# Second-conv results of the last image kept in SBUF, and the last stage's blocks in a mixed order

## The chip, the cores and the metric

The kernel runs on one core of a Trainium2 chip. The metric is the device time of one execution in microseconds (us). Three runs of the kernel before took 4049.6, 4058.78 and 4061.14 us; the median is 4058.78. The profiled execution spans 4055.7 us.

## The reference

Two layers run on x of shape (4, 128, 128, 128): four images of 128 channels and 128 x 128 pixels. Layer 0 is a windowed attention block followed by a depthwise-convolution MLP; it is not touched here. Layer 1 is a residual block with quantized 3x3 convolutions, and the change is in its last third:

```python
identity = x
out = act_quant(x)
out = conv3x3(out, weight_quant(w1))
out = batchnorm(out, gamma1, beta1)     # mean and variance over batch and pixels
out = act_quant(out)
out = conv3x3(out, weight_quant(w2))
out = batchnorm(out, gamma2, beta2)
return out + identity
```

The batchnorm is what shapes the kernel: no output of the second convolution can be scaled before the mean and variance over all four images are known.

## The kernel before, in words

The channels lie on the 128 partitions. Layer 1 cuts each image into 32 blocks of 4 rows, so that a block is 128 channels x 512 pixels: [...]256 KB in float32. Four images make 128 blocks. A convolution of one block (`conv3x3`, L783) is nine matmuls of 128x128 weights on 128x512 pixels, all in fp8, accumulated in one of four PSUM tiles (`ps_c`, L773).

Layer 1 runs in three stages after layer 0.

- The first-conv stage (L835 to L863) finishes layer 0 block by block, writes its result to HBM as the identity (`id_d`), quantizes it, convolves it with `wq[0]`, takes the statistics of the result (`stats_of`, L793) and copies the result out of PSUM (L829). For images 0 to 2 the copy goes on to HBM (`c1_d`). For image 3 it stays in SBUF, in `c1_s` (L800), 64 KB on each partition.
- The second-conv stage (L885 to L898) takes each first-conv result, from HBM or from `c1_s`, applies batchnorm and relu on ACT (L889), quantizes it in two DVE instructions (L890, L891) into padded fp8 images `q2` that stay in SBUF, and convolves each block with `wq[1]`, for the statistics alone (L896, L898): the results are thrown away. The last statistics feed the batchnorm's scale and shift (L900), a chain of small DVE and POOL instructions.
- The last stage (L913 to L922) convolves all 128 blocks a second time with the same `q2` and `wq[1]`. ACT applies scale and shift to the PSUM tile and writes `z` to SBUF (L918), DVE adds the identity (L919), and a DMA writes the block to the output (L920). The identity blocks come from HBM by `load_id` (L905).

`z`, the identity tile `idt` and the tiles of the second-conv stage come from the pool `ew` with three buffers each (L871). Identity loads are asked for two blocks ahead. Loads and writes of this stage are all issued by SyncE, in order, from one queue.

The order of the instructions on each engine in these stages is not the order of the program text: a scheduler arranges them when the kernel is built. For the second-conv stage it puts on ACT first all 96 relus that read loaded blocks and then all 32 that read `c1_s`. In the last stage SyncE's instructions alternate, one write and one load. Earlier parts (the attention) are arranged by hand; they don't concern the change.

Of the kernel before, what the change touches and what calls it, by code (L numbers as in the profile page):

```python
# [10 lines left out]
AF = mybir.ActivationFunctionType  # L11
# [3 lines left out]
P = 128  # L15
# [6 lines left out]
RB = 4  # L22
NBLK = P // RB
# [18 lines left out]
def layers(  # L42
# [29 lines left out]
    nc = tc.nc  # L72
    B = x.shape[0]
# [65 lines left out]
    with (  # L139
# [19 lines left out]
        for w in (wqkv, wp0.rearrange("p h m -> p (h m)")):  # L159
            n = w.shape[1]  # L160
# [41 lines left out]
    wq, kscale = [], []  # L202
# [28 lines left out]
    with (  # L231
# [27 lines left out]
        for n in range(3 * 32):  # L259
            s, ro, eo = n // 32, n % 32 // 2, n % 2  # L260
            m = ms[n % 4]
# [25 lines left out]
    with ExitStack() as actx:  # L287
# [352 lines left out]
        def beside(t):  # L640

            one = ln1_chunks(t + 1) if t + 1 < T else []
            two = post_chunks(t - 1) if t else []
            if t >= 2:
                b, i = bands[t - 2]
                if i == 4:
                    todo.extend(conv_steps(2 * b))
                    share[0] = -(-len(todo) // 4)  # L650
                elif i == NR - 1:
                    todo.extend(conv_steps(2 * b + 1))
                    share[0] = -(-len(todo) // 5)
            conv = [todo.pop(0) for _ in range(min(share[0], len(todo)))]
            n = max(len(one), len(two), 1)
            conv_of = [conv[len(conv) * c // (2 * n + 2) : len(conv) * (c + 1) // (2 * n + 2)] for c in range(2 * n + 2)]
            steps = []
            for c in range(n + 1):
                first = one[c] if c < len(one) else [None] * 4
                second = two[c] if c < len(two) else [None] * 5  # L660
                before = two[c - 1] if 0 < c <= len(two) else [None] * 5
                steps += [first[0]]
                if c:
                    steps += [second[0], before[3], *conv_of[2 * c], first[1], second[1], before[4]]
                else:
                    steps += [*conv_of[0], first[1], second[0]]
                steps += [*conv_of[2 * c + 1]]
                if c:
                    steps += [second[2], first[2], first[3]]
                else:  # L670
                    steps += [first[2], second[1], first[3], second[2]]
            return [s for s in steps if s]
# [6 lines left out]
        with nullcontext() if safe else tc.manual_schedule(engines=MANUAL):  # L679
# [5 lines left out]
            for t in range(T):  # L685
# [3 lines left out]
                side, at = beside(t), 0  # L689
                for j in range(NR):  # L690
# [5 lines left out]
                    for half in range(2):  # L696
# [3 lines left out]
                        at = upto  # L700
# [10 lines left out]
    def batchnorm(stats, n, gamma, beta, ks, name):  # L711

        mv = const.tile([P, n, 2], F32, name=f"mv{name}")
        for h in range(n):
            nc.vector.bn_aggr(mv[:, h, :], stats[h].rearrange("p c s -> p (c s)"))
        return affine(mv[:, :, 0], mv[:, :, 1], n, gamma, beta, ks, name)
# [53 lines left out]
    st2 = const.tile([P, B * NBLK, 6], F32, name="st2")  # L770
# [4 lines left out]
    def padded(pool, name):  # L775
        q = pool.tile([P, QW, QW], F8, name=name)
        nc.gpsimd.memset(q[:, 0, :], 0.0)
        nc.gpsimd.memset(q[:, QW - 1, :], 0.0)
        nc.gpsimd.memset(q[:, 1 : QW - 1, 0:1], 0.0)
        nc.gpsimd.memset(q[:, 1 : QW - 1, QW - 1 :], 0.0)  # L780
        return q

    def conv3x3(q, w, k):  # L783
        pc = ps_c.tile([P, RB, P], F32, name="pc")
        for t in range(9):
            dy, dx = divmod(t, 3)
            nc.tensor.matmul(  # L787
                pc, w[:, t, :], q[:, k * RB + dy : k * RB + dy + RB, dx : dx + P],
                start=(t == 0), stop=(t == 8),
            )  # L790
        return pc

    def stats_of(st, n, pc):  # L793
        nc.vector.bn_stats(st[:, n, :], pc.rearrange("p r c -> p (r c)"))  # L794

    blocks = [(b, k) for b in range(B) for k in range(NBLK)]
# [3 lines left out]
    c1_s = q1p.tile([P, P * P], F32, name="c1_s")  # L800
# [69 lines left out]
    q2 = [padded(q1p, f"q1_{b}") for b in range(B)]  # L870
    ew = ctx.enter_context(tc.tile_pool(name="ew", bufs=3))  # L871
    firsts = {}

    def load_first(n):
        b, k = blocks[n]
        px = slice(k * RB * P, (k + 1) * RB * P)
        if b == B - 1:
            firsts[n] = c1_s[:, px]
            return
        firsts[n] = ew.tile([P, RB * P], F32, name="c1l")  # L880
        nc.sync.dma_start(out=firsts[n], in_=c1_d[b][:, px])

    load_first(0)
    load_first(1)
    for n, (b, k) in enumerate(blocks):  # L885
        if n + 2 < len(blocks):
            load_first(n + 2)
        a = ew.tile([P, RB * P], F32, name="a")
        nc.scalar.activation(a, firsts.pop(n), AF.Relu, bias=sh1, scale=sc1)  # L889
        nc.vector.tensor_scalar(a, a, 15.0, ROUND, ALU.min, ALU.add)  # L890
        nc.vector.tensor_scalar(  # L891
            q2[b][:, 1 + k * RB : 1 + (k + 1) * RB, 1 : 1 + P],
            a.rearrange("p (r c) -> p r c", c=P), ROUND, None, ALU.subtract, saturate=False,
        )
        if k:
            stats_of(st2, n - 1, conv3x3(q2[b], wq[1], k - 1))  # L896
        if k == NBLK - 1:
            stats_of(st2, n, conv3x3(q2[b], wq[1], k))  # L898

    sc2, sh2 = batchnorm([st2], 1, ga2, be2, kscale[1], "2")  # L900

# [3 lines left out]
    def load_id(n):  # L905
        b, k = blocks[n]
        t = ew.tile([P, RB * P], F32, name="idt")
        nc.sync.dma_start(out=t, in_=id_d[b][:, k * RB * P : (k + 1) * RB * P])
        idt[n] = t

    load_id(0)
    load_id(1)
    for n, (b, k) in enumerate(blocks):  # L913
        if n + 2 < len(blocks):
            load_id(n + 2)
        pc = conv3x3(q2[b], wq[1], k)
        z = ew.tile([P, RB * P], F32, name="z")
        nc.scalar.activation(z, pc.rearrange("p r c -> p (r c)"), AF.Identity, bias=sh2, scale=sc2)  # L918
        nc.vector.tensor_tensor(z, z, idt.pop(n), ALU.add)  # L919
        nc.sync.dma_start(  # L920
            out=out[b, :, k * RB : (k + 1) * RB, :].rearrange("c r w -> c (r w)"), in_=z
        )  # L922
# [3 lines left out]
def conv_seq_kernel(tc: tile.TileContext, *args: bass.AP):  # L926
    nc = tc.nc
    with tc.tile_pool(name="flag", bufs=1) as fp:
        flag = fp.tile([1, 1], mybir.dt.int32, name="flag")
        layers(tc, False, flag, *args)  # L930


        large = nc.values_load(flag[0:1, 0:1])
        with tc.If(large > 0):
            layers(tc, True, flag, *args)
# [34 lines left out]
```

## Time and profile before

The stages of layer 1, from the trace (us from the start of the span; busy times in us):

| stage | from | to | PE busy | ACT busy | DVE busy | DMA share, GB/s |
|---|---|---|---|---|---|---|
| first conv | 2940 | 3524 | 518.3 of 584 | 397.1 | 308.4 | 0.87, 285 |
| second conv, its beginning | 3524 | 3560 | 31.8 of 36 | 20.5 | 27.6 | 0.60, 177 |
| second conv, while blocks are loaded | 3560 | 3670 | 99.9 of 110 | 73.6 | 96.5 | 0.56, 165 |
| second conv, after the loads | 3670 | 3740 | 70.0 of 70 | 7.2 | 33.3 | 0.00, 1 |
| second conv, its end | 3740 | 3803 | 63.0 of 63 | 0.0 | 25.6 | 0.00, 1 |
| last stage | 3810 | 3850 | 40.0 of 40 | 17.0 | 15.2 | 0.87, 288 |
| last stage, near its end | 3950 | 4000 | 50.0 of 50 | 19.5 | 18.0 | 0.84, 270 |

The first `z` of the last stage starts at 3803.25 us, the last at 4046.82, and the span ends at 4055.7. In the second-conv stage nothing but TensorE limits the time from 3670 on, with the DMA engines idle.

How to read the views: a group's line names the kernel's line, the engine and operation, output and inputs, the shapes and the count; then busy time in us, mean ns of one, idle time before them and what ended it. In the waits a row gives who waited for whom, the total in us, how many times, and the longest. Chain and timeline give the start and length in us of each piece of work. In a table of stretches "PEclk" is the share of full clock that TensorE was granted, and the DMA share is the mean busy share of the core's 16 DMA engines.

### The profile page before, as it was taken

The page shows a single profiled execution, that of the slowest core. Times are in us where ns is not written, and L with a number is a line of the kernel's source. Part 1 is how long each engine was busy: PE and PEld are TensorE (multiplying, and loading weights), DVE is VectorE, ACT ScalarE, POOL GpSimd, SP SyncE. Part 2 cuts the span into 40 slices and gives each one's busy share as a digit, 9 for nine tenths or more (in the row PEclk, how much of TensorE's full clock was granted, in tenths as well). Part 3 has the DMA queues.
Part 4 walks back from the last instruction along what each step waited for, and adds up shares of the span by engine and source line. Part 5 has one row for each costly group of instructions (what it writes and reads, how often), then busy time and mean ns, then how long its engine had stood idle before and what let it go on. Part 6 is the DMA issues. An engine that isn't in the chain of part 4 may idle for free.

```text
span 4055.7 us, 87210 instructions
## 1 busy us (share of the span) xinstructions
PE 3762.9 (93%) x35916; PEld 1914.1 (47%) x35916; DVE 1826.5 (45%) x3358; ACT 2326.4 (57%) x3534; POOL 384.2 (9%) x1381
## 2 busy tenths in 40 slices
PE   7699999999999999999999999997688889999999
PEld 5355455555555555555545555553333333334444
DVE  5244444444444444444444444442245555685433
ACT  3367666666666666666666666653156667662233
POOL 0011110111110010111110111100011111100000
PEclk9999999999999999999999999998579999999999
DMA  1223266676656657655666764657888889760487
GB/s 39 108 62 80 73 135 149 146 143 152 148 116 141 148 134 159 150 140 110 150 147 139 160 146 118 144 129 162 182 255 300 295 297 304 231 199 1 137 271 250
DMA packets 782938, 643.68 MB, mean 159 GB/s; under 512 B 572736, under 2 KB 585664, under 8 KB 782528
## 3 DMA queue, kind: packets, MB, share of 16 engines
q1 hardware_dynamic: 782528, 637.98, 60.8%
q8 instruction: 286, 4.69, 0.5%
q14 instruction: 124, 1.02, 0.1%
HBM read 365.07 MB, written 272.76 MB: 157 GB/s over the span
## 4 chain that ended last, share of the span: by engine, by line
PE 76%; DMA 9%; ACT 4%; issue 3%; DVE 3%; POOL 2%; SPq 2%; ACTq 0%; POOLq 0%; DVEq 0%
PE po L615 14%; PE pc L787 12%; PE pm L496 9%; PE sc L561 8%; PE pm L306 6%; PE pm L382 6%; PE pm L313 6%; PE pm L437 5%; DMA cv<-cv_d 3%; PE pm L549 3%; PE pb L849 3%; PE pm L420 2%; PE pw L269 2%; DMA c1l<-c_d 2%; DMA u<-y_d 2%
## 5 line engine op out<-in xcount | busy, mean ns | idle before, releaser
L628 DVE RECIPROCAL rd<-po 128x256 f32<-128x256 f32 x324 | 569.6, 1758 | 633.4 <-PE po L615 633.4
L787 PE MATMUL pc<-q,wq 128*128 128x512 fp8e4 x3456 | 794.5, 382 | 23.3 <-DVE st L794 9.4
L569 ACT ACTIVATE pt<-sc 128x1024 f32<-128x1024 f32 x648 | 627.2, 1019 | 58.0 <-PE sc L561 47.1
L787 PEld LDWEIGHTS <-wq 128*128 128x128 fp8e4 x3456 | 337.4, 98 | 517.5 <-issue 151.6
L496 PE MATMUL pm<-u,w 40*32 40x256 f32 x12288 | 454.6, 410 | 57.4 <-DMA u<-y_d 44.7
L507 DVE BATCH_NORM_STATS2 st<-c 128x6 f32<-128x256 f32 x512 | 181.4, 414 | 469.4 <-ACT c L505 468.9
L561 PE MATMUL sc<-q,kr 32*128 32x256 f32 x5184 | 373.6, 401 | 0.0
L496 PEld LDWEIGHTS pm<-u,w 40*32 40x32 f32 x12288 | 258.7, 112 | 240.8 <-issue 112.2
L505 ACT COPY c<-pm 128x512 f32<-128x512 f32 x256 | 139.0, 588 | 386.8 <-PE pm L496 377.8
L615 PE MATMUL po<-pt,v 128*32 128x256 f32 x5184 | 346.9, 385 | 0.0
L615 PE MATMUL po<-pt,ones 128*32 128x256 f32 x5184 | 339.1, 379 | 0.0
L561 PEld LDWEIGHTS sc<-q,kr 32*128 32x128 f32 x5184 | 233.9, 184 | 218.7 <-issue 181.3
L313 PE MATMUL pm<-sq,avg 128*128 128x512 f32 (+1 forms) x576 | 281.9, 571 | 31.7 <-ACT sq L308 27.0
L443 ACT ACTIVATE y<-pm,bp 128x512 f32<-128x512 f32 (+1 forms) x288 | 183.4, 641 | 222.9 <-PE pm L437 111.9
L849 PE MATMUL pb<-ge,wp 128*128 128x512 f32 x512 | 265.6, 614 | 46.6 <-ACT ge L846 46.5
L382 PE MATMUL pm<-xn,wqkv 128*128 128x512 f32 (+1 forms) x576 | 269.2, 570 | 15.6 <-DVE xn L318 15.6
L437 PE MATMUL pm<-xn,wp 128*128 128x512 f32 (+1 forms) x576 | 268.9, 559 | 5.7 <-DVE xn L318 5.7
L841 ACT ACTIVATE ge<-cv,shift,scale 128x512 f32<-128x512 f32 x256 | 202.8, 844 | 111.2 <-DMA cv<-cv_d 107.2
L308 ACT ACTIVATE sq<-pm 128x512 f32<-128x512 f32 (+1 forms) x288 | 157.2, 546 | 187.8 <-PE pm L306 187.7
L794 DVE BATCH_NORM_STATS2 st<-pc 128x6 f32<-128x512 f32 x256 | 177.8, 696 | 189.3 <-PE pc L787 189.2
L918 ACT ACTIVATE z<-pc,shift,scale 128x512 f32<-128x512 f32 x128 | 99.3, 777 | 269.0 <-PE pc L787 130.1
L315 ACT ACTIVATE rstd<-pm,eps_t 128x512 f32<-128x512 f32 (+1 forms) x288 | 184.3, 640 | 120.3 <-PE pm L313 114.7
(143 smaller groups left out, 4026.0 us busy)
## 6 DMA issues: line engine op xcount, KB each, us to landing
u<-y_d SPq DMA_DIRECT2D x128, 528.0 KB
cv_d<-c SPq DMA_DIRECT2D x512, 128.0 KB
cv<-cv_d SPq DMA_DIRECT2D x128, 512.0 KB
y_d<-y SPq DMA_DIRECT2D x224, 264.0 KB
w<-dw_d SPq DMA_DIRECT2D x64, 768.0 KB
xfl<-xf_d SPq DMA_DIRECT2D x128, 256.0 KB
id_d<-y SPq DMA_DIRECT2D x128, 256.0 KB
idt<-id_d SPq DMA_DIRECT2D x128, 256.0 KB
```

Source lines behind the costliest of these rows:

```text
L306: nc.tensor.matmul(pc[:, :n], center, src(), start=True, stop=True)
L313: nc.tensor.matmul(pv[:, :n], avg, held["sq"][:, :n], start=True, stop=True)
L382: nc.tensor.matmul(pm[:, : n * P], wqkv[:, m * P : (m + 1) * P], held["xn"][:, : n * P], start=True, stop=True,)
L437: nc.tensor.matmul(pm[:, : n * P], wp0[:, h, :], held["xn"][:, : n * P], start=True, stop=True)
L496: nc.tensor.matmul(pc[half][32 * q : 32 * q + 32, j, :].rearrange("p (g x) -> p g x", g=4), wt[hs, c, s, :], ut[hs, :, c, s : s + 64], sta ...
L561: nc.tensor.matmul(sc[h // 2][:, h % 2, kc, :].rearrange("p (r c) -> p r c", c=RS), region(kr, j)[hs, kc * P : (kc + 1) * P], queries(j, h ...
L569: nc.scalar.activation(pt, sc[p], AF.Exp)
L615: nc.tensor.matmul(po[hs, m, :], ones if m else v[:, kc, hs], pt[h // 2][:, h % 2, kc, :], start=(kc == 0), stop=(kc == 1),)
L628: nc.vector.reciprocal(rd, po[:, 1, :])
L787: nc.tensor.matmul(pc, w[:, t, :], q[:, k * RB + dy : k * RB + dy + RB, dx : dx + P], start=(t == 0), stop=(t == 8),)
L841: nc.scalar.activation(ge[:, h, :].rearrange("p (r c e) -> p r e c", r=RB, e=2), cv[:, h, :].rearrange("p (r e c) -> p r e c", r=RB, e=2), ...
L849: nc.tensor.matmul(pb, wp2[:, h, :], ge[:, h, :], start=(h == 0), stop=(h == 1))
```

## The change

`c1_s`, the SBUF room of image 3's first-conv results, is free once the second-conv stage has read them. The change uses it again. When the second-conv stage convolves a block of image 3, ACT copies the result from PSUM to that block's place in `c1_s`. In the last stage image 3 is then not convolved again: ACT reads its blocks from `c1_s`. So that the kept blocks don't come all at the end, the last stage goes through an order in which three computed blocks of images 0 to 2 are followed by one kept block of image 3, 32 times over. It is meant to relieve TensorE in the last stage.

```diff
+    def second_conv(n):
+        b, k = blocks[n]
+        pc = conv3x3(q2[b], wq[1], k)
+        stats_of(st2, n, pc)
+        if b == B - 1:
+            nc.scalar.copy(
+                c1_s[:, k * RB * P : (k + 1) * RB * P], pc.rearrange("p r c -> p (r c)")
+            )
...
         if k:
-            stats_of(st2, n - 1, conv3x3(q2[b], wq[1], k - 1))
+            second_conv(n - 1)
         if k == NBLK - 1:
-            stats_of(st2, n, conv3x3(q2[b], wq[1], k))
+            second_conv(n)
...
-    load_id(0)
-    load_id(1)
-    for n, (b, k) in enumerate(blocks):
-        if n + 2 < len(blocks):
-            load_id(n + 2)
-        pc = conv3x3(q2[b], wq[1], k)
+    order = [m for k in range(NBLK) for m in (*range((B - 1) * k, (B - 1) * (k + 1)), (B - 1) * NBLK + k)]
+    load_id(order[0])
+    load_id(order[1])
+    for at, n in enumerate(order):
+        b, k = blocks[n]
+        if at + 2 < len(order):
+            load_id(order[at + 2])
+        if b < B - 1:
+            pc = conv3x3(q2[b], wq[1], k).rearrange("p r c -> p (r c)")
+        else:
+            pc = c1_s[:, k * RB * P : (k + 1) * RB * P]
         z = ew.tile([P, RB * P], F32, name="z")
-        nc.scalar.activation(z, pc.rearrange("p r c -> p (r c)"), AF.Identity, bias=sh2, scale=sc2)
+        nc.scalar.activation(z, pc, AF.Identity, bias=sh2, scale=sc2)
```

In the changed kernel the copy stands at L879, the relu at L898, and `z`, the add and the write at L933 to L935.

## The prediction

> **What bounds the kernel now.** I read the chain of waits of the last 265 us first, since the change touches only the end of the program. Columns: start in us, length in us, what.
>
> ```profile
> 3789.86 256.93 PE pc L787 x1184
> 4046.79 0.02 issue
> 4046.82 0.79 ACT z L918
> 4047.60 0.02 issue
> 4047.62 0.69 DVE z L919
> ```
>
> The last stage is one unbroken run of matmuls on TensorE, then one block's scale-and-shift (ACT), one add (DVE), and 8.9 us from the last z at 4046.82 to the end of the span at 4055.7, in which the last writes land. So TensorE sets the end. Two groups of the page size the work:
>
> ```profile
> L918 ACT ACTIVATE z<-pc,shift,scale 128x512 f32<-128x512 f32 x128 | 99.3, 777 | 269.0 <-PE pc L787 130.1
> L794 DVE BATCH_NORM_STATS2 st<-pc 128x6 f32<-128x512 f32 x256 | 177.8, 696 | 189.3 <-PE pc L787 189.2
> ```
>
> ACT and DVE each need under 0.8 us of a block. Next the waits of the last stage, its first 35 us and then the rest (waiter, releaser, us in total, times, longest):
>
> ```profile
> ACT z L918 <- DMA out_dram<-z: 13.5, 12, 2.1
> DVE z L919 <- ACT z L918: 10.6, 12, 2.1
> DVE z L919 <- DMA idt<-id_d: 9.9, 6, 2.7
> ACT z L918 <- PE pc L787: 5.8, 6, 1.2
> ```
> ```profile
> DVE z L919 <- ACT z L918: 136.0, 108, 1.6
> ACT z L918 <- PE pc L787: 125.5, 107, 1.2
> ACT z L918 <- DMA out_dram<-z: 1.5, 1, 1.5
> ```
>
> These two differ in kind, and the forecast rests on that. When the batchnorm is ready at 3803.25, TensorE has run four blocks ahead (four accumulators), so the first z's don't wait for matmuls. They wait for z buffers whose write hasn't landed (12 times) and for identity loads (6 times). Only when ACT has used up that lead is it TensorE that ends the wait, 107 times of 108. The first 25 us thus show the stage without its TensorE limit. In the timeline (start, length, instruction, idle before and releaser):
>
> ```profile
> 3807.03 0.78 ACT L918 ACTIVATE z<-pc,shift,scale 128x512 f32<-128x512 f32 x1 [1.67 <-DMA out_dram<-z]
> ...
> 3828.63 0.78 ACT L918 ACTIVATE z<-pc,shift,scale 128x512 f32<-128x512 f32 x1 [0.66 <-DMA out_dram<-z]
> ...
> 3830.10 0.78 ACT L918 ACTIVATE z<-pc,shift,scale 128x512 f32<-128x512 f32 x1 [0.69 <-PE pc L787]
> ```
>
> The z at 3807.03 is the fourth, that at 3828.63 the sixteenth: 21.60 us / 12 = 1.80 us a block. Without the first step (2.44 us, the queue filling up; the fifth z starts at 3809.47) it is 19.16 / 11 = 1.74. From 3830.10 to 4046.82 the other 111 blocks take 216.72 us, 1.95 each: nine matmuls of 217 ns. Last, busy time by stretch (us; PE, PEld, DVE, ACT, POOL with counts; clock, DMA share, GB/s):
>
> ```profile
> 3300.00:3400.00 100.00, 89.32 (x298) 35.29 (x297) 51.90 (x90) 68.84 (x92) 13.52 (x22) 1.00 0.89 298
> 3807.00:3829.00 22.00, 22.00 (x104) 9.85 (x102) 8.31 (x12) 9.70 (x13) 0.00 (x0) 1.00 0.90 304
> 3838.00:4046.80 208.80, 208.78 (x963) 93.36 (x960) 74.11 (x107) 83.03 (x107) 0.00 (x0) 1.00 0.84 269
> ```
>
> At TensorE's pace the DMA engines already stand at 84% and 269 GB/s. Freed of it they reach 90% and 304 GB/s, the level of the first-conv stage (298), which often waits for its loads. The room below TensorE is some 12%, not the 25% of matmuls that go.
>
> **What the Trainium skill says.** "DMA: Bandwidth & Descriptors", Anatomy of one DMA: about 2 us of a transfer are fixed, mostly the write's receipt (fitted there for the GpSimd path). The trace agrees in kind: the stage's first 256 KB write is issued at 3804.78 and frees its buffer at 3807.03, 2.25 us; under load issue to reuse is 2.8 to 5.3 us. "HBM Reference", Specifications: about 358 GB/s per core. The trace has 359 for one 4 us stretch (3807 to 3811) but holds 304 over 22 us; the measured figure is used. "TensorE: Matmul & The Clock Gate", Part 1: the clock halves after an idle window of about 3.4 us. The trace has 0.50 from 2860 to 2980 us, where TensorE is idle a third of the time, and 1.00 from 3300 to 3400, where it is 89% busy.
>
> **The change, part by part.**
>
> 1. *Matmuls removed.* The last image's 32 blocks are not convolved again: 32 x 9 = 288 matmuls, 32 x 1.95 = 62.4 us of TensorE, all on the chain. TensorE then needs 96 x 1.95 = 187 us, or 5.86 us for each group of three computed blocks and a kept one (1.46 us a block).
>
> 2. *Copies added.* 32 ACT copies of 128x512 from PSUM in the second-conv stage. The same copy in the first-conv stage (L829) has a median of 577 ns: 18.5 us of ACT. ACT is idle there: between 3670 and 3740 it is busy 7.15 us, from 3740 to 3803 not at all, and the last image's convolutions fall at 3803 - 32 x 1.95 = 3741 and later. In program order each copy would stand ahead of the next relu (L889), and the relu's block feeds the next convolution, which would tie ACT to TensorE block by block; in the order as built all 128 relus come first and then the 32 copies, so nothing but copies is queued behind a copy that waits. Each copy follows its block's statistics (L829 does so too), so an accumulator is held 0.70 + 0.58 = 1.28 us after its last matmul; with four of them TensorE needs it back only after three more blocks, 5.9 us. The last copy runs beside the batchnorm, whose steps on DVE and POOL take from 3797.54 to 3803.15. Cost: nothing. The copy overwrites first-conv results that ACT has read by 3679.
>
> 3. *Loads and writes.* The same 128 loads and 128 writes of 256 KB, the same three buffers of each, the same alternation on the queue (write, load, write, load), only in another order of blocks. A kept block reads SBUF in place of PSUM: the relu from this buffer (L889) takes 808 ns against the 777 of z, 32 x 0.03 = 1 us, hidden under the waits.
>
> 4. *What sets the pace then.* A z buffer goes through ACT 0.78, DVE 0.69, then issue to reuse, mean 3.58 us over the ten writes issued from 3809.5 to 3824.9: with handovers about 5.15, and with a third to half a us of the waits for loads 5.3 for three blocks, 1.77. By bandwidth: 2 x 262,144 bytes at 304 GB/s are 1.72 us, at 298 1.76. By count, 1.74 to 1.80. I take 1.76; ends 1.68 (the 312 GB/s held from 3020 to 3060) and 1.86 (282 GB/s).
>
> Sum: the fourth z stays at 3807.03 (it waits for the first write, as now). The 128th comes 124 x 1.76 = 218.2 us later, at 4025.3, against 4046.8; the 8.9 us tail stays. Saved: 21.5 us. From 4058.8 that gives 4037; with 1.68 4027, with 1.86 4050. TensorE, needing 1.46 of 1.76 us, is 83% busy and has the rest to make up delays.
>
> **Rivals.**
>
> *A, the transfers keep up.* If the queue fills the DMA engines (304 / 0.90 = 338 GB/s), a block takes 1.55 us and the last z comes at 3807.03 + 192.2 = 3999: 48 us less, 4011. The 359 GB/s of one 4 us stretch speak for it; against it, 304 over 22 us with ACT already waiting for buffers, and 298 over a long stage that has larger loads.
>
> *B, a wait takes the matmuls' place.* Reads and writes come in bunches (2.9 us issue to reuse for one write, 5.3 for another 2.7 us later). If three buffers settle into the bad phase, a block costs about 1.95 us as now: 4058, no change. Nearby traffic that ran at 304 speaks against it.
>
> *C, slower.* TensorE now pauses in every group. If it lost half its clock for a third of the stage, three blocks would take 9 x 3 x 0.43 = 11.6 us, 2.9 for each of 43 blocks: 43 x 2.9 + 85 x 1.76 = 274 us against 250, so 24 us slower, 4083. The 0.50 clock before 2980 speaks for it; against it, the pauses would be 4 x 1.76 - 5.86 = 1.2 us, and the first-conv stage at 87 to 89% busy holds 1.00. A copy that blocked relus would end on this side too, but the order as built excludes it.
>
> **How the numbers follow.** Main case 78%, A 9%, B 8%, C 5%. The time is the main case's, 4037. The range goes from 4023, a little into A, to 4050, where B begins. Faster by over 0.3% (below 4046.6) is A and the main case up to 1.84 us a block: 0.86; within 0.3%: 0.09; slower: 0.05.
>
> **What would show it.** Right: the last stage's chain alternates z, add and DMA in place of one matmul run; ACT's z waits chiefly for the write of z and DVE for idt; DMA share near 0.90 and 295 to 312 GB/s up to the end; z spacing near 1.76 us; TensorE about 83% busy at clock 1.00; 32 copies from about 3741 with TensorE unbroken up to 3803, and the first z still at 3803. Wrong: gaps in TensorE before 3803 (step 2), a spacing near 1.46 with ACT waiting for pc (step 4, towards A) or near 1.95 at less than 280 GB/s (B), a clock below 0.9 (C).

## Result and profile after

The changed kernel takes 4039.66 us (median of six runs, 4026.91 to 4043.68), against a forecast of 4037 with a range of 4023 to 4050. With three more runs of the kernel before, its median is 4051.57. The ratio is 0.9958, with a 95% interval of 0.9938 to 0.9978: 17 us less, between 9 and 25. Both kernels scatter by more than 10 us, and part of that has nothing to do with the change. In the two profiled runs the first-conv stage starts at 2978.9 us before and at 2984.0 after, though the change touches no instruction ahead of it. So the stage itself is the finer measure.

The waits of the last stage (waiter, releaser, us in total, times, longest):

```profile
ACT z L933 <- DMA out_dram<-z: 100.7, 104, 2.5
DVE z L934 <- DMA idt<-id_d: 83.3, 61, 2.6
DVE z L934 <- ACT z L933: 55.0, 65, 2.6
...
PE pc L787 <- ACT z L933: 27.9, 34, 2.0
...
ACT z L933 <- PE pc L787: 3.3, 3, 2.2
```

Before, ACT waited 107 times of 108 for TensorE once the first 35 us were over. Now it does so three times in the whole stage, and 104 times it waits for a write to land and give back its z buffer. TensorE in turn waits for ACT to give back an accumulator. The instructions of z and the copies (duration min/median/max in ns, first and last start in us):

```profile
L933 ACT ACTIVATE z<-pc,shift,scale x96: 769/777/778, 3807.2 to 4030.0; 128x512 f32<-128x512 f32 x96
L933 ACT ACTIVATE z<-c_s,shift,scale x32: 812/812/815, 3811.5 to 4032.4; 128x512 f32<-128x512 f32 x32
L879 ACT COPY c_s<-pc x32: 585/585/586, 3741.0 to 3801.6; 128x512 f32<-128x512 f32 x32
```

From first to last z the stage takes 4032.4 - 3807.2 = 225.2 us, where it took 4046.8 - 3803.2 = 243.6. From the fourth z (3811.52) to the last (4032.39) a block costs 220.87 / 124 = 1.78 us.

Where these 1.78 us come from can be read off the single instructions (means over blocks 11 to 110). A z buffer's round is 0.79 us on ACT, 0.31 until its add starts (chiefly the wait for the identity load), 0.69 for the add, 0.03 to the issue of the write, and 3.49 from there until ACT fills the buffer again: 5.31 us. An identity buffer's round is as long, within 0.01: 0.69 for the add, 0.42 to the issue of the next load, 4.19 from there to that load's add. Three buffers share a round, so a block takes 5.31 / 3 = 1.77 us. The queue hardly holds the writes back, as the 0.03 us show.

Busy time by stretch (us; PE, PEld, DVE, ACT, POOL with counts; clock, DMA share, GB/s):

```profile
3740.00:3803.00 63.00, 63.00 (x292) 28.23 (x291) 23.84 (x33) 18.73 (x32) 0.00 (x0) 1.00 0.00 1
...
3829.00:4032.00 203.00, 168.51 (x747) 72.39 (x746) 79.18 (x115) 90.31 (x115) 0.00 (x0) 0.99 0.91 296
```

The 18.7 us of copies leave TensorE unbroken. In the last stage it is busy 168.51 of 203 us, 83%, at a clock of 0.99, while the DMA engines move 296 GB/s at a share of 0.91. In the profiled pair 18.4 us come off the stage, 0.5 go to a longer tail (9.4 us for 8.9), and 4.0 to the later first z: 13.9, the difference of the two spans.

### The profile page after: what moved, and what is told of

Its sections match the earlier page's. It is cut to its first block, busy times and chain, and to the rows that moved or that the text cites. A ratio compares the mean times of both kernels' runs of the same rounds, so it can differ in the third digit from the quotient of the medians.

```text
span 4041.8 us, 86698 instructions
## 1 busy us (share of the span) xinstructions
PE 3712.2 (92%) x35628; PEld 1887.7 (47%) x35628; DVE 1825.2 (45%) x3358; ACT 2345.4 (58%) x3566; POOL 382.8 (9%) x1381
## 5 line engine op out<-in xcount | busy, mean ns | idle before, releaser
L787 PE MATMUL pc<-q,wq 128*128 128x512 fp8e4 x3168 | 737.4, 381 | 51.8 <-ACT z L933 27.9
L787 PEld LDWEIGHTS <-wq 128*128 128x128 fp8e4 x3168 | 308.7, 98 | 517.8 <-issue 190.6
L549 PEld LDWEIGHTS pm<-wqkv,yr 128*128 128x128 f32 x1296 | 193.6, 191 | 122.4 <-issue 117.5
```

The source lines that it names most:

```text
L549: nc.tensor.matmul(pv[:, c, :], region(yr, j)[:, c * P : (c + 1) * P], wqkv[:, 2 * P :], start=True, stop=True)
L787: nc.tensor.matmul(pc, w[:, t, :], q[:, k * RB + dy : k * RB + dy + RB, dx : dx + P], start=(t == 0), stop=(t == 8),)
```

## The experiments

What was open was why a block costs 1.78 us. The forecast had two counts for it that gave the same number, three buffers waiting for their own landings and DMA engines near their limit, and did not separate them. The diffs below are against the changed kernel unless another is named. "Stage" is the time from first to last z in the profiled run; each ratio is to runs of the kernel before on the same chip, with its 95% interval. The runs were made in three batches on three chips, so between batches compare stages and ratios, not times.

### The copies alone

```diff
-    order = [m for k in range(NBLK) for m in (...)]
+    order = list(range(len(blocks)))
...
-        if b < B - 1:
-            pc = conv3x3(q2[b], wq[1], k).rearrange("p r c -> p (r c)")
-        else:
-            pc = c1_s[:, k * RB * P : (k + 1) * RB * P]
+        pc = conv3x3(q2[b], wq[1], k).rearrange("p r c -> p (r c)")
```

> The 32 copies are made in the second-conv stage, but nothing reads them: the last stage convolves all 128 blocks in their old order. My theory (copies lie in idle ACT time): TensorE unbroken from 3670 us to the last matmul, first z about 282.8 us after the first-conv stage's batchnorm as before, last stage 243.6 us from first to last z, time within 2 us of the kernel before. Rival (copies hold accumulators or delay the statistics): gaps in TensorE before the first z and up to 32 x 0.58 = 18.5 us more.

Measured: stage 243.6 us, ratio 0.9994 (0.9986 to 1.0003). "Batchnorm" below means the start of the last step of layer 1's first batchnorm, its shift. From there to the first z it takes 277.1 us, 277.4 before. TensorE is busy throughout:

```profile
3665.00:3791.00 126.00, 126.00 (x582) 56.51 (x581) 51.94 (x79) 20.84 (x35) 0.55 (x1) 1.00 0.00 1
```

The copies cost nothing.

### The kept blocks at the end

```diff
-    order = [m for k in range(NBLK) for m in (...)]
+    order = list(range(len(blocks)))
```

> As the changed kernel, but the last stage keeps the old order, so the 32 kept blocks come last. My theory (transfers pace a block at 1.78 us, TensorE at 1.95): first z to fourth 4.3 us, 13 blocks at 1.78, 80 at 1.95, 32 kept ones at 1.78, together about 240 us from first to last z, against 225 of the changed kernel and 243.6 of the one before; so mixing is worth about 15 us of it. Rival (kept blocks pass quicker when no matmuls run beside them, at 1.46 to 1.55 us): 230 us, and mixing is worth little.

Measured: stage 235.6 us, ratio 0.9971 (0.9954 to 0.9987). Once TensorE's lead is used up, the z's of the computed blocks come 1.95 us apart again; those of the kept blocks come 53.7 / 31 = 1.73 us apart:

```profile
L933 ACT ACTIVATE z<-c_s,shift,scale x32: 812/812/814, 3973.1 to 4026.8; 128x512 f32<-128x512 f32 x32
```

So kept blocks go hardly quicker when TensorE is idle: what paces them is not on TensorE. With three buffers the mixed order is worth 235.6 - 225.2 = 10.4 us of the stage's 18.4, less than the 15 that were expected.

### Six buffers of each kind

```diff
+    ez = ctx.enter_context(tc.tile_pool(name="ez", bufs=6))
+    ei = ctx.enter_context(tc.tile_pool(name="ei", bufs=6))
-        t = ew.tile([P, RB * P], F32, name="idt")
+        t = ei.tile([P, RB * P], F32, name="idt")
-    load_id(order[0])
-    load_id(order[1])
+    for m in order[: 6 - 1]:
+        load_id(m)
-        if at + 2 < len(order):
-            load_id(order[at + 2])
+        if at + 6 - 1 < len(order):
+            load_id(order[at + 6 - 1])
-        z = ew.tile([P, RB * P], F32, name="z")
+        z = ez.tile([P, RB * P], F32, name="z")
```

> The changed kernel with six buffers in place of three for z and for the identity blocks (and so three more identity blocks loaded ahead of the last stage). Theory 'bandwidth' (the 16 DMA engines are the bound at 296 to 300 GB/s): spacing of z stays at 1.72 to 1.78 us, only the three loads ahead save 2 to 3 us, DMA share 0.90 to 0.95. Theory 'buffers' (three buffers in flight are too few, each waits for its own landing): DMA share near 1.00, about 330 GB/s, spacing 1.55 to 1.60 us, some 25 us saved in the stage; ACT waits mostly for TensorE or DVE.

Measured: 3991.78 us, ratio 0.9845 (0.9825 to 0.9865); stage 181.7 us, 1.43 us a block. The waits and the traffic:

```profile
ACT z L935 <- PE pc L787: 81.6, 87, 1.2
...
ACT z L935 <- DMA out_dram<-z: 4.1, 6, 1.5
DVE z L936 <- DMA idt<-id_d: 0.8, 1, 0.8
```
```profile
3804.00:3980.00 176.00, 176.00 (x813) 78.82 (x812) 83.36 (x121) 91.20 (x120) 0.00 (x0) 1.00 1.01 365
```

The same loads and writes on the same engines run at 365 GB/s, and TensorE sets the end again. The 296 GB/s of the changed kernel are not what the DMA engines can do. They are what three buffers can ask for. This settles the question for buffers, and by more than that theory expected. The edit also gives z and the identity blocks a pool each, but that alone is not what does it: the two runs with six buffers of one kind have the same pools and stay above 215 us.

### No identity loads

```diff
     load_id(order[0])
-    load_id(order[1])
+    same = idt[order[0]]
...
-        if at + 2 < len(order):
-            load_id(order[at + 2])
...
-        nc.vector.tensor_tensor(z, z, idt.pop(n), ALU.add)
+        nc.vector.tensor_tensor(z, z, same, ALU.add)
```

> The changed kernel without the identity loads of the last stage, all but the first: DVE adds the same identity block to every z, so the identity of the other blocks is left out; adds, z and writes are as they were. My theory (reads and writes share the DMA engines, and the write's landing is long because of the loads): a write lands in about 2.3 us, the z loop takes (0.78 + 0.69 + 2.3 + 0.1) / 3 = 1.29 us, so TensorE is the bound again at 1.46 us a block, 187 us from first to last z, DMA about 180 GB/s. Rival (the write's landing takes 3.6 us by itself): spacing stays near 1.73 us, 219 us.

Measured (one run): 3985.58 us, stage 182.0 us. With three z buffers as in the changed kernel:

```profile
ACT z L931 <- PE pc L787: 62.9, 68, 1.2
ACT z L931 <- DMA out_dram<-z: 22.9, 16, 2.7
```

TensorE sets the pace here: a z buffer's round is short enough when no loads run beside the writes. The 16 writes that ACT waited for took 2.69 us from issue to reuse in the mean; beside the loads, in the changed kernel, the 104 waited for took 3.51. Part of the gain is that the adds no longer wait for loads; the run with six identity buffers, below, shows that this part alone is not enough.

### Six buffers of one kind only

The same edit for z alone (identity left at three), and for the identity alone (z left at three).

> The changed kernel with six z buffers and three identity buffers as it had. Theory 'two loops' (z buffers and identity buffers each pace the stage by their own landing times, with nearly the same period): ACT stops waiting for the write of z, DVE's wait for the identity load takes its place, spacing only down to 1.60 to 1.70 us, last stage 205 to 218 us from first to last z. Rival 'z loop alone' (only the write's landing binds): TensorE the bound as with six of both, 1.42 us, 182 us.

> The changed kernel with six identity buffers and three z buffers as it had. Theory 'two loops': DVE stops waiting for identity loads, ACT's wait for the write of z stays, spacing 1.60 to 1.72 us (the z loop, 0.78 + 0.69 + about 3.6 us over three buffers), last stage 205 to 220 us. Rival 'load loop alone': TensorE the bound, 182 us.

Measured: with six z buffers the stage takes 219.6 us from first to last z, ratio 0.9936 (0.9917 to 0.9955); with six identity buffers 216.0 us, ratio 0.9937 (0.9920 to 0.9955). Both intervals overlap that of the changed kernel (0.9938 to 0.9978), so the stages have to tell. The waits, first with six z buffers, then with six identity buffers:

```profile
DVE z L936 <- DMA out_dram<-z: 84.7, 81, 2.5
ACT z L935 <- DMA out_dram<-z: 68.0, 63, 3.3
DVE z L936 <- DMA idt<-id_d: 47.7, 40, 3.0
```
```profile
ACT z L935 <- DMA out_dram<-z: 101.0, 110, 2.2
DVE z L936 <- DMA idt<-id_d: 19.1, 13, 2.1
```

With six z buffers the time to the last z misleads, because ACT now runs further ahead of the adds. The adds themselves, first in the changed kernel, then with six z buffers (duration min/median/max in ns, first and last start in us), show it:

```profile
L934 DVE TENSOR_TENSOR z<-z,idt x128: 691/693/694, 3808.0 to 4033.2; 128x512 f32<-128x512 f32 x128
L936 DVE TENSOR_TENSOR z<-z,idt x128: 691/693/694, 3800.8 to 4025.8; 128x512 f32<-128x512 f32 x128
```

From first to last add it is 225.2 us and 225.0 (in the other runs this count and the stage agree within 1 us): six z buffers alone bring nothing, and ACT, three blocks further ahead, still waits for writes. Six identity buffers alone bring 9 us of the 43.5 that both bring. So two loops pace the stage. The identity loop alone keeps it at 5.31 / 3 = 1.77 us; with that loosened, the z loop, whose round is then 5.11 us, holds it at 1.70. The theory of two loops was right, but it expected the z buffers alone to help. With six z buffers the profile often puts DVE's wait down to a write that the add does not use. At those adds z had been ready for at least 3.98 us, so the other input, the identity load, is the likely cause; it was not tried.

### Four buffers of each kind

> The changed kernel with four z and four identity buffers. With three of each a buffer's round took 3 x 1.78 = 5.34 us. If the landing times stay as they were, four buffers give 5.34 / 4 = 1.34 us a block, below TensorE's 1.42: TensorE the bound, 182 us from first to last z, as with six. If landing grows with the load (Little's law at a fixed transfer rate of 300 GB/s, against which the six-buffer run's 366 GB/s already speaks), spacing between 1.45 and 1.75 us, 185 to 222 us.

Measured: 3989.52 us, ratio 0.9855 (0.9833 to 0.9878); stage 185.5 us, 1.46 us a block:

```profile
3800.00:3960.00 160.00, 159.44 (x735) 71.27 (x733) 75.64 (x110) 85.99 (x110) 0.00 (x0) 1.00 1.00 359
```

One buffer more of each kind, 4 KB on each partition, gives nearly all of it. The result lies between the two expectations. The landing did not stay as it was: the 112 writes that ACT still waits for (75.8 us in all) took 4.17 us from issue to reuse, 3.51 in the changed kernel, so that a block costs 1.46 us and not the 1.34 that the buffers alone would allow. But the traffic was not fixed at 300 GB/s either, and TensorE is busy 159.44 of 160 us.

### Six buffers in the kernel before

The six-buffer edit, with no block kept.

> The kernel before with six z and six identity buffers, no block kept. My theory (there TensorE paces the stage at 1.95 us a block, and buffers count only for the first sixteen blocks): last stage 243 us from first to last z as before, time within 3 us of the kernel before; so the 60 us of the six-buffer run are the product of both edits. Rival (buffers alone bring most of it): 20 us less or more.

Measured: stage 243.5 us, as before; ratio 1.0012 (1.0005 to 1.0019), a little slower.

```profile
L920 ACT ACTIVATE z<-pc,shift,scale x128: 769/777/782, 3798.4 to 4041.9; 128x512 f32<-128x512 f32 x128
```

Where TensorE paces the stage, buffers alone buy nothing. The gain of six buffers exists only with the change.

### The kept blocks at the end, with six buffers

> The six-buffer version with the kept blocks at the end (old order). My theory: TensorE paces the first 96 blocks at 1.95 us (less the four it is ahead), about 181 us, in which the DMA engines have room that is not used; then 32 kept blocks go as fast as the DMA engines allow, 1.35 to 1.45 us at 365 to 389 GB/s, 43 to 46 us; about 226 us in all, against 182 mixed. So the mix is worth 44 us with six buffers where it was worth 10 with three. Rival (kept blocks without matmuls run at ACT's 0.82 us): 207 us.

Measured: ratio 0.9952 (0.9933 to 0.9971), stage 220.7 us against 181.7 mixed. A stretch with matmuls, then one in which only kept blocks are left:

```profile
3810.00:3970.00 160.00, 160.00 (x739) 71.75 (x738) 56.75 (x82) 63.61 (x83) 0.00 (x0) 1.00 0.85 270
3978.00:4012.00 34.00, 0.00 (x0) 0.00 (x0) 18.68 (x27) 21.23 (x27) 0.00 (x0) 0.50 1.03 386
```

The mix is worth 39 us with enough buffers. At the end, a kept block takes (4015.4 - 3976.4) / 31 = 1.26 us, quicker than the 1.35 to 1.45 expected. The traffic of 386 GB/s would give 1.36 us for a load and a write; the first kept blocks had their loads in already.

### More in flight in the other two stages

The first run takes the six-buffer version and gives the first-conv stage four buffers in place of three for its loads, and for the result `y` that it writes, which comes from the same pool. The second adds six buffers for the loads of the second-conv stage.

```diff
-        tc.tile_pool(name="ld", bufs=3) as ld,
+        tc.tile_pool(name="ld", bufs=4) as ld,
-        load(0)
-        load(1)
+        for m in range(4 - 1):
+            load(m)
-            if n + 2 < len(blocks):
-                load(n + 2)
+            if n + 4 - 1 < len(blocks):
+                load(n + 4 - 1)
```

> The six-buffer version, and in the first-conv stage four buffers in place of three for its loads (cv, the attention result and y) with loads asked for three blocks ahead. The stage now runs at 4.2 us a block with the DMA engines at 0.90 and 300 GB/s, the same mark as the last stage had with three buffers. If that mark is again too few transfers in flight: above 320 GB/s and 3.7 to 4.0 us a block (nine matmuls of 0.217 and four of 0.43 us are 3.67 us of TensorE), 30 to 65 us less than the six-buffer run. If the stage is held by the order of its queue or by TensorE: within 10 us of the six-buffer run.

Measured: 3974.38 us, ratio 0.9816 (0.9797 to 0.9835). From the first load-fed activation to the next batchnorm the stage takes 532.3 us, where the six-buffer run had 548.2.

```profile
3010.00:3390.00 380.00, 349.38 (x1177) 143.49 (x1176) 206.88 (x363) 278.00 (x362) 60.69 (x103) 1.00 0.93 310
```

310 GB/s in place of 299: the stage was held by its buffers too, but 16 us are half of the least that was expected if that were all. They are also not exact: in the eleven profiled runs that leave this stage as it was it takes 541.2 to 548.3 us, so the gain is 9 to 16. What holds it beyond that (its queue issues loads and writes in order) was not separated.

```diff
+    el = ctx.enter_context(tc.tile_pool(name="el", bufs=6))
-        firsts[n] = ew.tile([P, RB * P], F32, name="c1l")
+        firsts[n] = el.tile([P, RB * P], F32, name="c1l")
-    load_first(0)
-    load_first(1)
+    for m in range(5):
+        load_first(m)
-        if n + 2 < len(blocks):
-            load_first(n + 2)
+        if n + 5 < len(blocks):
+            load_first(n + 5)
```

> The six-buffer version with deeper loads in the first-conv stage, and now also six buffers in place of three for the first-conv results that the second-conv stage loads, asked for five blocks ahead. The second-conv stage takes 276 us from its batchnorm to the next one's first z; 128 blocks at 1.95 are 250 us, the fill and the batchnorm some 15. If its loads hold it back in its first 130 us (TensorE was 88 to 91% busy there): 8 to 12 us less than the run without this edit, so about 3964. If DVE, with three instructions per block, holds it: within 3 us of it.

Measured: 3956.66 us, ratio 0.9771 (0.9752 to 0.9789), the fastest version of all. Batchnorm to first z falls from 276.2 us in the run above to 261.6: 14.6 us, more than the 8 to 12 expected if the loads held the stage back. The early part of the second-conv stage, first in the changed kernel, then here:

```profile
3560.00:3670.00 110.00, 100.24 (x445) 42.86 (x443) 95.95 (x231) 73.00 (x93) 0.00 (x0) 1.00 0.60 172
```
```profile
3530.00:3640.00 110.00, 110.00 (x509) 49.31 (x507) 99.47 (x250) 74.15 (x95) 0.00 (x0) 1.00 0.45 145
```

TensorE, 91% busy before, has no gaps left. A DMA share of 0.60 had hidden a stage that waited for its loads.

## Why the prediction was right, and where its reasoning was not

The time lies in the range, 2.7 us from the forecast, and the gain has the forecast sign. That the time is so near is partly luck: the forecast took 21.5 us from 4058.8, the median of three runs, and with three more that median is 4051.57, from which the same step gives 4030. The gains are the fair comparison: 21.5 us forecast, 17 (9 to 25) measured, 18.4 in the stage. By steps:

- **Matmuls removed.** Right: TensorE is busy 83% as worked out, and the feared loss of clock did not come (0.99).
- **Copies at no cost.** Right, shown by the run with the copies alone; their 585 ns match the 577 of the copy they were priced by. That they start at 3741.0, as forecast, is chance. The forecast counted 32 convolutions back from the first z, 5.7 us after the last statistics; in the trace before, the statistics of image 3's first block end at 3737.0, and the trace after runs 4.0 us later.
- **Loads and writes, kept blocks read from SBUF.** Right: 812 against 777 ns.
- **The pace.** 1.78 us against 1.76, read off the first 25 us of the last stage before. The stage's gain is 18.4 us for the forecast 21.5: 124 x 0.02 = 2.5 in the pace and 0.6 in the first three blocks; 0.5 more went to the tail. The measured ratio's 17 us agree with that.
- **The buffer's round.** The mechanism was right: buffers that wait for their landings, with some wait for loads. The sum was not: 5.15 us plus "a third to half a us" is 5.5 to 5.65, not 5.3, and would have given 1.83 to 1.88 us. Measured, the round is 5.31, since the handovers, the waits for loads and the write's landing were each a little shorter than assumed. The forecast stood on the spacing read off the old trace, not on this sum.
- **What sets the pace.** Here the step "By bandwidth: 2 x 262,144 bytes at 304 GB/s are 1.72 us, at 298 1.76" failed. That it agreed with the buffer count was no second witness: 304 GB/s was itself the traffic of three buffers. So was, in part, the first-conv stage's 298, which the prediction called as a witness; it rose to 310 with one buffer more.
- **"The room below TensorE is some 12%, not the 25% of matmuls that go"** was near for this kernel, where 1.95 to 1.78 us is 9%, but it is not the room of the DMA engines. With one buffer more of each kind nearly the whole 25% is there: 243.6 to 185.5 us is 24%.
- **Rivals.** A, "the transfers keep up", was rejected because ACT already waited for buffers at 304 GB/s. Those waits were the reason that the traffic stayed at 304. A's own figure, 338 GB/s from 304 / 0.90, was too low: 365 were reached with TensorE as the bound and 386 with it out of the way. B and C did not come. C's sum compares 274 us with 250, though the stage took 243.6; it would have cost 30 us, not 24.

## What to carry to other kernels

When work is taken off the bounding engine, look at the part of the old trace where that engine has a lead: the waits there are those of the next bound, and their spacing is the new pace. If those waits are for buffers, work out the buffer's round (compute, issue, landing) and divide by the count before believing in a bandwidth limit, since a rate measured behind too few buffers is the buffers' rate. Try one more buffer of every kind in the round together; one kind alone shows little (here nothing and 9 us, of 43.5). Measure a stage by the same point of the work in all versions, here the adds: an engine that only runs further ahead looks like a gain.

## What the runs showed of the hardware that was not expected

- The DMA share does not tell how much room is left. It read 0.91 at 296 GB/s and 1.01 at 365; taken as a linear scale, 0.91 would have put the limit at 325.
- One core with one issuing queue moved 386 GB/s of mixed loads and writes in 256 KB pieces for 34 us. The Trainium skill's "HBM Reference" (Specifications) gives about 358 GB/s as the share of a core and adds that a core streaming alone measures above it; the trace agrees with the addition, and the 358 that the prediction named is no ceiling here.
- Landing depends on what runs beside it. A 256 KB write took 2.25 us from issue to reuse when it met an idle queue, 2.69 in the mean with no loads beside the writes, 3.51 (2.22 to 5.34) beside the loads at 296 GB/s, and 4.17 at 359 GB/s with four buffers.
- The prediction quotes an idle window of about 3.4 us for the halving of TensorE's clock. In the traces shorter pauses were followed by it: in the second-conv stage of the kernel before, one of 2.66 us from 3622.2, with a clock of 0.50 from 3625.4 to 3628.9; in the six-buffer run with the kept blocks at the end, one of 1.89 us from 3135.2, with 0.50 from 3138.3 to 3141.7. The pauses of the changed kernel's last stage, up to 1.95 us, were not followed by it. So rival C was nearer than its 1.2 us of pause made it look; what decides was not tried.
